# A sparse two-layer graph kernel: value gathers that add into the rows of x while they land

## The chip, the cores and the metric

The kernel runs on one core of a Trainium2 chip. The metric is the device time of one launch in microseconds (us); lower is better. Three runs of the kernel before gave 1190.85, 1191.04 and 1189.97 us, a median of 1190.85 us.

## The reference

Two graph layers over 4096 nodes with 512 features and a random sparse adjacency (some ten neighbours a node). What matters, cut short:

```python
h = jnp.maximum(_layernorm(x), 0.0)
Q, K, V = (h @ W.T for W in (WQ, WK, WV))           # 8 heads of 64
attn = softmax(Q @ K^T * SCALING + energy, masked by adj)
hard = (attn == attn.max(-1, keepdims=True)) / 8      # the best neighbour of each head
x = x + einsum('hqk,hkd->hqd', hard, V)               # layer 0
h = jnp.maximum(_layernorm(x), 0.0)
agg = (adj > 0) @ h / degree
x = x + relu(concat(h @ W_self + b_self, agg @ W_nb + b_nb) @ W_comb + b_comb)   # layer 1
```

Layer 0 gives each node, for each of eight heads, the value row of its single best neighbour, divided by eight. So layer 0 is a search for the best neighbour and a sum of x with eight slices of 64 values. That sum is what the change is about.

## The kernel before

It has three stages.

1. **Lists (0 to about 305 us).** The adjacency is packed into words and decoded to lists of neighbours. Keys, values, x and some per-row numbers (the list, its length, the layernorm's scale and shift) go to one wide table in DRAM, `K_d`: a row holds value, key, numbers, x. The nodes are sorted by degree, so that the 32 tiles of 128 nodes have capacities from 24 neighbours down to 5 (`CAPS`, L512).
2. **Layer 0 and the products of layer 1 (about 305 to 905 us).** A loop over `i` from -5 to 31 (L1652) takes the tiles in the order `turns`: 0, 1, 24, 2, 25, 3, 26, 14, 4, 27, 5, 15, 6, 16, 7, and so on, the last four being 28 to 31. In step `i` it scores the tile `turns[i]` and does earlier or later work of other tiles.
3. **Aggregation (about 905 us to the end).** Rows of `G_d` (layer 1's neighbour product, written in stage 2) are gathered and summed on VectorE for 24 tiles, eight tiles are summed by TensorE through 0/1 masks, and the output is written.

In stage 2 the tiles are of two kinds. The 14 tiles of large capacity (0 to 13) are **apart**: only keys are gathered for their neighbours, and the values are fetched after the winners are known, with eight indirect gathers of 128 rows by 64 floats, one for each head (`value_gathers`, L1221). The other 18 are **fused**: key and value come in one gather of 1025 floats, and the winners are picked by predicated copies on VectorE (L1290).

The names and lines that the steps below touch:

- `rows(r)`, L1162: gathers the tile's own rows, called in step `i` for `turns[i + 5]`. For 25 of the tiles they land in `km`, a tile of 1088 floats a row out of a ring of **eight** (`bufs=8`, L1171). It holds the key, the numbers and, in its last 512 columns, x itself; these columns are called `xg`. The other seven (`wide`) tiles use a part of `room`.
- `query_norm`, L1175: ScalarE reads the list, the numbers and `xg`.
- `scores`, L1238, `winners`, L1266: VectorE multiplies and reduces, group by group of up to four neighbours, then finds the best. For an apart tile the result is `vi`, the row numbers for the value gathers (L1312).
- `value_gathers`, L1221: eight gathers into columns of `o`, a ring of three. They are queued on POOL alternately with the key gathers of a later step (L1671 to L1676).
- `layer1_xo`, L1315: VectorE adds `xg` and `o` into `xo` (L1318, 128 by 512), and SyncE stores `xo` to `X1_d` (L1319). Called by `layer1_stats`.
- `layer1_stats`, L1321: ScalarE sums `xo` (L1332), its squares (L1333) and takes the square root (L1334).
- `layer1_inverse`, L1346: one reciprocal on VectorE (L1348). It is recorded inside `scores` of the same step, behind the first group of neighbours.
- `layer1_norm`, L1350: five ScalarE instructions, L1355 to L1359; the last one reads `xo` and writes the normalised row. It is the last reader of `xo`.
- `layer1_turn`, `layer1_copy`, `layer1`: transposes and products of layer 1.

Every engine works its instructions in the order recorded here (`manual_schedule`), and semaphores keep the order between engines. A tile taken from a ring waits until all readers of an earlier holder of its place are done, also where these are recorded later in the same step. POOL issues the indirect gathers one after another from one queue; a waiting gather holds up all behind it. On that queue each gather also waits for the one eight places before it to have landed, because there are eight semaphores for it.

The order of a step, shortened:

```python
a, b = on(key_gathers, i), late(value_gathers, "value", i)   # POOL
on(rows, i + 5)                                              # POOL: a km from the ring
...
if i >= 0 and turns[i] in fused:
    own_values(turns[i])                                     # POOL
...
late(layer1_stats, "stats", i)                               # VectorE sum, ScalarE sums
...
scores(turns[i], within)                                     # VectorE; the reciprocal inside
on(winners, i)
late(layer1_norm, "stats", i)                                # ScalarE
```

The `plan` (L1591) says in which step a tile has its stats: tiles 0, 24, 1, 25, 2, 26, 3 in steps 3 to 9, and so on, one in a step.

Of the kernel before, what the change touches and what calls it, by code (L numbers as in the profile page):

```python
# [9 lines left out]
F32 = mybir.dt.float32  # L10
# [3 lines left out]
ALU = mybir.AluOpType  # L14
# [4 lines left out]
P = 128  # L19
D = 512  # L20
NC = D // P
H = 8
HD = D // H
# [502 lines left out]
def stats_of(nc, pool, x, mv):  # L526

    st = pool.tile([P, 6], F32, tag="st_s", name="st_s")
    nc.vector.bn_stats(st, x)
    nc.vector.bn_aggr(mv, st)  # L530
# [14 lines left out]
def sparse_path(  # L545
# [4 lines left out]
    nc = tc.nc  # L550
# [560 lines left out]
    with ExitStack() as pb:  # L1111
        bp = pb.enter_context(tc.tile_pool(name="sb", bufs=2))
        xp = pb.enter_context(tc.tile_pool(name="sbx", bufs=8))
# [6 lines left out]
        def gather(dst, src, idx, at=0):  # L1120
            last[0] = nc.gpsimd.indirect_dma_start(  # L1121
                out=dst, out_offset=None, in_=src,
                in_offset=bass.IndirectOffsetOnAxis(ap=idx, axis=0), element_offset=at,
            )
            if at:

                beyond.append(last[0])
                for w in written:
                    tc.declare_no_dep(last[0].ins, w.ins, reason="other columns")
# [32 lines left out]
        def rows(r):  # L1162

            if r in wide:
                k = (wide.index(r) - len(wide)) % OWNS
                own = big[:, OWN0 + k * VKX : OWN0 + (k + 1) * VKX]
                gather(own, K_d[:, :], perm[:, r : r + 1])
                km = own[:, D:VKX]
                st[r]["own"] = own
            else:  # L1170
                km = xp.tile([P, ROWX], F32, tag="km", name="km", bufs=8)  # L1171
                gather(km, K_d[:, :], perm[:, r : r + 1], D)
            st[r].update(km=km, xg=km[:, M_X:ROWX])
# [46 lines left out]

        def value_gathers(r):  # L1221
            s = st[r]
            s["o"] = xp.tile([P, D], F32, tag="o", name="o", bufs=3)
            return [(s["o"][:, ts(h, HD)], V_h, s["vi"][:, h : h + 1]) for h in range(H)]


        V_h = K_d.rearrange("n (a d) -> (n a) d", d=HD)

        def own_values(r):

            s = st[r]
            if r in wide:
                s["o"] = s["own"][:, 0:D]
            else:
                s["o"] = xp.tile([P, D], F32, tag="o", name="o", bufs=3)
                gather(s["o"], K_d[:, :], perm[:, r : r + 1])
# [77 lines left out]

        def layer1_xo(r):  # L1315
            s = st[r]
            s["xo"] = xp.tile([P, D], F32, tag="xo", name="xo", bufs=2)
            nc.vector.tensor_tensor(s["xo"], s["xg"], s["o"], ALU.add)  # L1318
            nc.sync.dma_start(X1_d[ts(r, P), 0, :], s["xo"])  # L1319

        def layer1_stats(r, by_vector=False):  # L1321

            s = st[r]
            if "xo" not in s:
                layer1_xo(r)
            xo = s["xo"]
            if not by_vector:

                q = bp.tile([P, 8], F32, tag="q1", name="q1", bufs=3)

                junk = bp.tile([P, D], F32, tag="hn1", name="hn1", bufs=3)
                nc.scalar.activation(junk, xo, AF.Copy, scale=-1.0 / D, accum_out=q[:, 0:1])  # L1332
                nc.scalar.activation(junk, xo, AF.Square, bias=q[:, 0:1], accum_out=q[:, 1:2])  # L1333
                nc.scalar.activation(q[:, 2:3], q[:, 1:2], AF.Sqrt, bias=epsb, scale=1.0 / D)  # L1334
                nc.scalar.activation(q[:, 3:4], q[:, 1:2], AF.Identity, bias=epsh, scale=-0.5 / D)
                s.update(xo=xo, sq=q, hn=junk)
                return
            mv = bp.tile([P, 2], F32, tag="mv1", name="mv1")
            stats_of(nc, bp, xo, mv)
            v = bp.tile([P, 1], F32, tag="v1", name="v1")  # L1340
            nc.vector.tensor_scalar(v, mv[:, 1:2], EPS, None, ALU.add)
            rs = bp.tile([P, 1], F32, tag="rs1", name="rs1")
            nc.scalar.activation(rs, v, AF.Sqrt)
            s.update(xo=xo, mv=mv, v=v, rs=rs)
# [307 lines left out]
        for i in range(-5, KT):  # L1652
# [16 lines left out]
            if i == 1:  # L1669
                wN = bp.tile([P, NC, D], F32, tag="swN", name="swN", bufs=1)  # L1670
            a, b = on(key_gathers, i), late(value_gathers, "value", i)  # L1671
            while a or b:
                for q, n in ((a, max(1, round(len(a) / max(1, len(b))))), (b, 1)):
# [26 lines left out]
            words_turn()  # L1700
            hot_some(i)
            late(layer1_stats, "stats", i)
            on(query_norm, i + 4)
            late(layer1_out, "move", i)
# [31 lines left out]
        for r in before:  # L1736
            layer1_turn(r)
            tail_turn(r)
        late(layer1_xo, "stats", KT)
        late(layer1_stats, "stats", KT, True)  # L1740
        late(layer1_norm, "stats", KT)
        for r in early[-1:]:
# [40 lines left out]
    with ExitStack() as pd:  # L1783
# [71 lines left out]
        s = ahead  # L1855
# [39 lines left out]
def kernel(tc, *args):  # L1895
    left = sparse_path(tc, *args)
    with tc.If(left > 0):
        general_path(tc, *args)
# [40 lines left out]
```

## Time and profile before

One execution was profiled. Its own time was 1188.29 us and its span 1186.5 us; the median of the three runs without a profile is 1190.85 us.

| What | us |
|---|---|
| Profiled execution, time | 1188.29 |
| Profiled execution, span | 1186.5 |
| TensorE busy over the span | 1023.9 (86%) |
| VectorE busy | 982.7 (83%) |
| POOL busy | 715.1 (60%) |
| ScalarE busy | 550.1 (46%) |
| 112 value gathers `o<-K_d,vi`, POOL busy | 108.1 |
| 32 sums `xo`, VectorE busy (25 from `km`, 7 from `room`) | 17.2 and 4.8 |

How to read the lines: engines are PE (TensorE), DVE (VectorE), ACT (ScalarE), POOL (GpSimd) and SP (SyncE). A line of the timeline has its start and length in us, the engine, the source line, the operation, and output<-inputs; in brackets stands the idle time of the engine just before, and what ended it. "issue" there means that the engine waited for nothing that the profile shows. Line numbers are those of the kernel before.

### The profile page before, as it was taken

The numbers are of one execution on the slowest core, as the hardware profiler recorded it, in microseconds if no ns is written. First come the engines' busy times: TensorE is split into PE (matmuls) and PEld (weight loads), VectorE is DVE, ScalarE is ACT, GpSimd is POOL, SyncE is SP. The second block draws the span as 40 slices with busy tenths as digits, with TensorE's granted clock in tenths as the row PEclk, the third lists the DMA queues.
The fourth block names the chain that finished last, engine by engine and source line by source line (L and its number), as shares of the span: only waits on it lengthen the run. The fifth ranks groups of instructions, "written<-read, shape, count | busy, mean of one in ns | idle before, by whom it ended". The sixth has DMA issues, their size and how long they took to land. (4 is left out here: it accounts for less than half of the span.)

```text
span 1186.5 us, 11454 instructions
## 1 busy us (share of the span) xinstructions
PE 1023.9 (86%) x3079; PEld 501.6 (42%) x3079; DVE 982.7 (83%) x1548; ACT 550.1 (46%) x1222; POOL 715.1 (60%) x939
## 2 busy tenths in 40 slices
PE   3999999979599668688879989888989999999792
PEld 1555555644244224344334434444434444444340
DVE  4358789889289798798989999999983699998894
ACT  3777777932222377486567678754462100000000
POOL 3332323312677757757777777777713777777774
PEclk9999999989799878889889889888999999999996
DMA  9999999979797678889898889988865888888973
GB/s 353 418 420 418 413 418 375 396 226 293 229 269 251 180 233 261 255 278 292 281 289 281 284 280 298 291 279 280 284 256 171 306 310 275 321 288 276 369 242 108
DMA packets 115594, 348.44 MB, mean 294 GB/s; under 512 B 21472, under 2 KB 23552, under 8 KB 107328
## 3 DMA queue, kind: packets, MB, share of 16 engines
q0 software_dynamic: 60560, 201.01, 53.0%
q1 hardware_dynamic: 50560, 146.56, 32.5%
q10 hardware_dynamic: 4400, 0.05, 0.3%
q8 instruction: 26, 0.43, 0.1%
q14 instruction: 48, 0.39, 0.1%
HBM read 287.75 MB, written 64.00 MB: 296 GB/s over the span
## 5 line engine op out<-in xcount | busy, mean ns | idle before, releaser
L1805 PE MATMUL da<-gk,mk 128*128 128x512 f32 x512 | 223.2, 599 | 6.9 <-DVE mk L1556 6.2
L1121 POOL DMA_INDIRECT room<-G_d,sidx x174 | 168.5, 969 | 84.6 <-issue 80.7
L636 PE MATMUL q<-wq,hqT 128*128 128x512 f32 x256 | 151.0, 745 | 51.3 <-DVE pr L1244 51.3
L1250 DVE TENSOR_REDUCE sc<-pr 128x32 f32<-128x2048 f32 (+3 forms) x114 | 183.3, 1608 | 3.8
L1121 POOL DMA_INDIRECT kg<-K_d,sidx x161 | 153.4, 953 | 49.0 <-issue 40.2
L1830 DVE TENSOR_REDUCE acc<-room 128x512 f32<-128x4096 f32 (+5 forms) x23 | 153.0, 6651 | 32.5 <-DMA room<-G_d,sidx 30.6
L1805 PEld LDWEIGHTS da<-gk,mk 128*128 128x128 f32 x512 | 98.2, 192 | 131.9 <-issue 123.1
L1121 POOL DMA_INDIRECT room<-K_d,sidx x118 | 111.6, 945 | 42.9 <-issue 25.6
L1121 POOL DMA_INDIRECT o<-K_d,vi x112 | 108.1, 965 | 34.2 <-issue 32.0
L636 PE MATMUL pk<-wk,room 128*128 128x512 f32 x256 | 118.5, 606 | 2.6 <-ACT room L821 2.6
L636 PE MATMUL pv<-wv,room 128*128 128x512 f32 x256 | 112.6, 592 | 0.0
L636 PEld LDWEIGHTS q<-wq,hqT 128*128 128x128 f32 x256 | 59.2, 243 | 123.0 <-issue 77.7
L1244 DVE TENSOR_TENSOR pr<-q,kg 128x2048 f32<-128x2048 f32 (+3 forms) x47 | 93.3, 1985 | 11.2 <-DMA kg<-K_d,sidx 10.1
L1393 PE MATMUL pr<-swS,hT 128*128 128x512 f32 x216 | 97.1, 592 | 0.0
L636 PE MATMUL pg<-swN,hT 128*128 128x512 f32 x216 | 97.1, 593 | 0.0
L760 ACT ACTIVATE mkt<-adjt,sgb 128x2048 bf16<-128x2048 int32 x44 | 88.0, 1999 | 2.1 <-POOL adjt L678 2.1
L1244 DVE TENSOR_TENSOR pr<-q,room 128x2048 f32<-128x2048 f32 (+3 forms) x42 | 73.2, 1744 | 18.1 <-DMA room<-K_d,sidx 16.0
L636 PEld LDWEIGHTS pv<-wv,room 128*128 128x128 f32 x256 | 48.3, 190 | 59.3 <-issue 59.1
L636 PEld LDWEIGHTS pk<-wk,room 128*128 128x128 f32 x256 | 47.5, 196 | 51.5 <-issue 47.8
L830 DVE SCALAR_TENSOR_TENSOR ks<-pk,swe 128x512 f32<-128x512 f32 x32 | 21.9, 686 | 52.5 <-PE pk L636 46.8
L1517 ACT ACTIVATE hot<-ramp,code 128x256 bf16<-128x256 bf16 x105 | 52.5, 500 | 22.5 <-DVE code L1498 22.5
L779 PE MATMUL pw<-mkt,planes 128*128 128x256 bf16 x512 | 62.8, 277 | 0.0
(254 smaller groups left out, 1619.5 us busy)
## 6 DMA issues: line engine op xcount, KB each, us to landing
adjt<-adj_dram SPq DMA_DIRECT2D x44, 1024.0 KB, 10.4
room<-adj_dram SPq DMA_DIRECT2D x20, 1024.0 KB, 11.0
x<-X_d SPq DMA_DIRECT2D x25, 512.0 KB, 7.8
xt<-x_dram SPq DMA_DIRECT2D x32, 256.0 KB, 8.1
K_d<-ks POOLq DMA_DIRECT2D x32, 256.0 KB, 6.5
X_d<-xo SPq DMA_DIRECT2D x32, 256.0 KB, 4.5
G_d<-gs SPq DMA_DIRECT2D x32, 256.0 KB, 3.9
gk<-G_d SPq DMA_DIRECT2D x16, 512.0 KB, 4.8
```

What stands on the lines that cost most here:

```text
L636: nc.tensor.matmul(dst, h[:, c, :], w[:, c, :], start=(c == 0), stop=(c == NC - 1))
L760: nc.scalar.activation(mk, st[t]["adj"][j], AF.Sigmoid, bias=sgb, scale=400.0, accum_out=degs[:, t, j : j + 1],)
L779: nc.tensor.matmul(pw, planes[:, s, :], st[t]["mk"][j][:, ts(i, SEG)], start=False, stop=(s == NPL - 1),)
L830: nc.vector.scalar_tensor_tensor(ks.rearrange("p (h d) -> p h d", h=H), st[t]["pk"].rearrange("p (h d) -> p h d", h=H), HD**-0.5, web.unsq ...
L1121: last[0] = nc.gpsimd.indirect_dma_start(out=dst, out_offset=None, in_=src, in_offset=bass.IndirectOffsetOnAxis(ap=idx, axis=0), element_o ...
L1244: nc.vector.tensor_tensor(pr[:, :g, :], s["q"].unsqueeze(1).to_broadcast([P, g, D]), kk[:, :, 0:D], ALU.mult)
L1250: nc.vector.tensor_reduce(sc[:, g0 : g0 + g, :], pr[:, :g, :].rearrange("p g (h d) -> p g h d", h=H), AX.X, ALU.add,)
L1393: nc.tensor.matmul(pr, s["hT1"][:, c, :], wS[:, c, :], start=False, stop=(c == NC - 1 and mine is None and not open_))
L1517: nc.scalar.activation(one, ramp, AF.Square, bias=code[:, 0, k : k + 1])
L1805: nc.tensor.matmul(dacc[r], masks[s][:, r, h, :], keys[s][:, h, :], start=(s == 0 and h == 0), stop=(s == NPL - 1 and h == 1),)
L1830: nc.vector.tensor_reduce(acc, g[:, 0:n, :].rearrange("p n f -> p f n"), AX.X, ALU.add)
```

## The change

The eight value gathers of an apart tile no longer write to a tile `o`. They are issued with an add as compute operation and land on the tile's own x, the columns `xg` inside its `km`. After the eight have landed, `xg` is the sum. The VectorE sum of these 14 tiles is left out, and so are their tiles `o` and `xo`. The store to `X1_d`, the three ScalarE readers of stats and norm now read `km`. The 18 fused tiles keep their sum. The store, up to now marked done by the presence of `xo`, is marked by `put`.

```diff
         def gather(dst, src, idx, at=0):
             last[0] = nc.gpsimd.indirect_dma_start(
                 out=dst, out_offset=None, in_=src,
+                **({"compute_op": ALU.add} if src is V_h else {}),
                 in_offset=bass.IndirectOffsetOnAxis(ap=idx, axis=0), element_offset=at,
             )
...
         def value_gathers(r):
             s = st[r]
-            s["o"] = xp.tile([P, D], F32, tag="o", name="o", bufs=3)
-            return [(s["o"][:, ts(h, HD)], V_h, s["vi"][:, h : h + 1]) for h in range(H)]
+            s["xo"] = s["xg"]
+            return [(s["xg"][:, ts(h, HD)], V_h, s["vi"][:, h : h + 1]) for h in range(H)]
...
         def layer1_xo(r):
             s = st[r]
-            s["xo"] = xp.tile([P, D], F32, tag="xo", name="xo", bufs=2)
-            nc.vector.tensor_tensor(s["xo"], s["xg"], s["o"], ALU.add)
+            if "xo" not in s:
+                s["xo"] = xp.tile([P, D], F32, tag="xo", name="xo", bufs=2)
+                nc.vector.tensor_tensor(s["xo"], s["xg"], s["o"], ALU.add)
             nc.sync.dma_start(X1_d[ts(r, P), 0, :], s["xo"])
+            s["put"] = True
 
         def layer1_stats(r, by_vector=False):
 
             s = st[r]
-            if "xo" not in s:
+            if "put" not in s:
                 layer1_xo(r)
```

## The prediction, made before the changed kernel ran

> **What bounds the kernel now.** I began with stage 2, where the change lies, and asked of each engine whether it waits. First the windows view (length, then busy time and count of PE, PEld, DVE, ACT, POOL, then clock, DMA share, GB/s).
>
> ```profile
> core 0: us, PE busy (x) PEld busy (x) DVE busy (x) ACT busy (x) POOL busy (x), PEclk, DMA share, GB/s
> ...
> 516.00:690.00 174.00, 146.38 (x413) 70.49 (x412) 160.82 (x194) 118.15 (x314) 131.91 (x139) 0.89 0.89 284
> 690.00:830.00 140.00, 124.62 (x342) 59.58 (x341) 134.25 (x174) 93.48 (x256) 106.17 (x112) 0.90 0.90 284
> ```
>
> POOL looks three quarters busy, but a gather of 0.945 us is always followed by 0.30 us of issue, and 139 x 1.25 = 174 us and 112 x 1.25 = 140 us: the queue has no gap between 516 and 830 us. VectorE is 92% and 96% busy in them. Two full engines, so the question is which one waits for the other. The timeline of POOL shows the gathers of own rows (`km`):
>
> ```profile
> 423.32 0.94 POOL L1121 DMA_INDIRECT km<-K_d,perm  x1 [6.80 <-DVE xo L1318]
> 441.18 0.94 POOL L1121 DMA_INDIRECT km<-K_d,perm  x1 [0.30 <-issue]
> ...
> 483.23 0.94 POOL L1121 DMA_INDIRECT km<-K_d,perm  x1 [0.30 <-issue]
> ...
> 516.02 0.94 POOL L1121 DMA_INDIRECT km<-K_d,perm  x1 [8.14 <-DVE xo L1318]
> ```
>
> The only two long holes of the queue between 342 and 859 us stand here: a row gather waits until the sum at L1318 has freed a place in the ring of `km`. And the timeline of VectorE shows its waits for gathers:
>
> ```profile
> 485.82 2.29 DVE L1244 TENSOR_TENSOR pr<-q,room 128x2048 f32<-128x2048 f32 x1 [5.09 <-DMA room<-K_d,sidx]
> ...
> 829.69 1.76 DVE L1244 TENSOR_TENSOR pr<-q,room 128x1536 f32<-128x1536 f32 x1 [1.06 <-DMA room<-K_d,sidx]
> ...
> 855.59 2.29 DVE L1244 TENSOR_TENSOR pr<-q,room 128x2048 f32<-128x2048 f32 x1 [0.35 <-DMA room<-K_d,sidx]
> ```
>
> At 855.59 VectorE still waits for a gather issued by a queue that has run without a gap since 516.02. So POOL sets the time up to there; then VectorE's last three and a half tiles end at 893, the last products follow, and the gathers of stage 3 start at 905.44. What moves POOL's start at 516 moves all of that, and stage 3 with it.
>
> **The change, part by part.**
>
> *Removed: 14 sums.* Each is 0.69 us by its row, 0.60 from its start to the next one's (436.88 to 437.48): 8.4 us of VectorE. Of these, 12 lie before 829.69, where VectorE then waits for a gather, so they lengthen a wait and give nothing. Two lie behind it (839.38 and one at 852.64), and the wait at 855.59 takes up those 1.2 us. I count 0; if POOL did not bind, it would be 8.4.
>
> *Removed: tiles `o` and `xo` of 14 tiles.* Gathers into `o` wait in the profile for nothing but issue (116 times 0.30 us), so their places are not short: 0.
>
> *Moved: the release of `km`.* Until now an apart tile's `km` is free after L1318. Now its last reader is the norm on ScalarE (L1359), and the store to `X1_d` reads it too. In the changed program as built, the row gathers of steps 3, 5, 7 and 9 wait for exactly this: the norm and the store of tiles 0, 1, 2 and 3, where they waited for the sum. (Step 4, the hole at 423.32, follows tile 24, which is fused: unchanged. Later apart holders have their stats steps ahead, and only their stores are waited for: 0.) The norm comes late because its reciprocal (L1348) stands on VectorE behind the first group of the step's scores:
>
> ```profile
> 443.44 0.15 DVE L1348 RECIPROCAL q<-q 128x1 f32<-128x1 f32 x1
> ...
> 515.07 0.68 DVE L1318 TENSOR_TENSOR xo<-km,o 128x512 f32<-128x512 f32 x1
> ...
> 521.64 0.15 DVE L1348 RECIPROCAL q<-q 128x1 f32<-128x1 f32 x1
> ```
>
> ```profile
> 444.94 0.81 ACT L1359 ACTIVATE hn<-xo,q 128x512 f32<-128x512 f32 x1
> ...
> 522.38 0.18 ACT L1355 ACTIVATE q<-q 128x1 f32<-128x1 f32 x1
> ...
> 523.67 0.81 ACT L1359 ACTIVATE hn<-xo,q 128x512 f32<-128x512 f32 x1
> ```
>
> - Step 3: tile 0's norm ends at 398.55, the gather is at 408.06. No wait.
> - Step 5: tile 1's norm ends at 445.75. Without the sum the reciprocal is 0.60 earlier: 445.15. From release to the gather's start POOL takes 0.27 (515.75 to 516.02). So 445.42 in place of 441.18: **+4.24 us**. The store, issued by 437.6 with 4.5 us to landing, is done before. Behind the gather wait the fused rows of step 6; VectorE waits for these by 466.98 (2.16 us, `o`), 476.06 (2.60) and 485.82 (5.09), so it slips by the same 4.24.
> - Step 7: POOL arrives at 487.47; tile 2's norm ended at 482.89, and 4.24 - 0.60 + 0.27 later is 486.8. No wait.
> - Step 9: the reciprocal at 521.64 becomes 521.64 + 4.24 - 0.60 = 525.28, ending 525.43. ScalarE waited 1.47 us for the sum in this step and no longer does, so its chain starts at once, 0.04 later; from L1355 to the norm's end it takes 524.48 - 522.38 = 2.10: 527.57, and POOL at 527.84 in place of 516.02. The stall has grown from 8.14 to 15.7, and the shift in all is **+11.8 us**, the 4.24 among it.
>
> Behind that gather wait the key gathers of tile 5 and then everything. VectorE has 9.3 us of waits between 529 and 830 and eight sums (4.8 us) less to do there, none of which helps a queue that is full.
>
> *Changed: 112 gathers add.* No row of this trace adds while landing. POOL's time for a gather doesn't follow the width (0.94 to 0.95 us for 64, 513 and 1088 floats), so an extra price would be one for each row's descriptors. From below: 0. From above, the nearest rows are two plain writes of 128 and of mostly 640 to 1024 rows:
>
> ```profile
> L729 POOL DMA_DIRECT2D K_d<-s x4: 548/554/582, 30.9 to 32.6; - x4
> ...
> L933 POOL DMA_DIRECT2D K_d<-meta x5: 929/944/997, 140.0 to 297.7; - x5
> ```
>
> (944 - 554) ns for 512 further rows is 0.76 ns a row, 0.10 us for 128. A farther bound is all that an indirect gather costs above a direct write, 0.945 - 0.554 = 0.39 us. I take the middle of 0 and 0.10, 0.05 us. On the path are 80 gathers behind 516, some 15 between 441 and 485, some 14 before 407: 109 x 0.05 = **+5.4 us** (0 to 10.9; by the far bound 42.5). The Trainium skill ("Collectives: The Full Stack", section "The bandwidth ceiling: the fold count and why AG ≠ RS ≠ AR") says that an add in the DMA needs two source reads and so two read descriptors for each chunk; it speaks against the change. Taken as an estimate with the row above, three descriptors in place of two are half a row's price, 64 x 0.76 = 0.05 us and 5.3 us in all; no run here shows it.
>
> Landing: value gathers land after 2.4 to 7.4 us (median 4.4), and the queue looks back eight gathers, 10.0 us. Their readers stand a step behind: tile 13's last gather lands near 847.5, its ScalarE sum was at 853.35. I count 0 up to a landing of 10 us.
>
> *Sum:* 11.8 + 5.4 = 17.2. On the profiled execution 1188.29 + 17.2 = 1205.5; on the median, 2.56 us above it, 1190.85 + 17.2 = **1208 us**. Its own range, from the two ends of the add's price: 1203 to 1214.
>
> **The rivals.**
>
> *The adds cost POOL far more, or land late.* For it: nothing in the trace shows an add, and the queue has no slack. Against it: width costs nothing now. At 0.39 us each, 11.8 + 42.5 gives 1245. If a landing took 12 us, the look back of eight would set a pace of 12/8 = 1.5 us for 160 gathers, the 80 value gathers behind 516 and as many between them: 0.25 x 160 = 40, and 1243.
>
> *VectorE takes up part of the stall.* For it: from 667.4 to 829.7 it never waits, so it might be the late one, and 8.4 us of its work goes. Then the end moves by 11.8 - 8.4 = 3.4: 1194. Against it: at 829.69 and 855.59 it waits for gathers, so its lead is nil there.
>
> *Faster: VectorE is the bound and the removed sums count in full.* One mechanism, at 516 to 830 us: 14 x 0.60 = 8.4, 1182. It decides if the row gathers don't wait longer, that is if the norms end before POOL reaches them (440.88) or where it already waits (515.75). They end at 445 and 524.
>
> **How the numbers follow.** Forecast 0.67; costlier or late adds 0.20, spread from 1214 up; VectorE takes up a part 0.08; faster 0.05. The range goes from 1197, which leaves out the faster case and half of the partial one, to 1236, which leaves out the upper half of the costly case: about 0.19 outside. A measurement of this kernel can tell 0.2%, some 2.4 us, from no change. Faster 0.05; within 0.2%: 0.03, from the partial case; slower 0.92.
>
> **What would show it.** Right: the row gather of step 5 begins behind ACT's norm with some 5 us idle, that of step 9 with 15 to 16; POOL without gaps after that; VectorE waits for `room` and `kg` more than 9 us longer in all; stage 3 starts some 17 us later and is as long as before; the value gathers at about 1.0 us. Wrong: row gathers without new waits, or a start of stage 3 that moves by less than 8 us. A value gather at 0.945 takes 5.4 us off the sum; one at 1.3 makes the second case.

## The result, and the profile after

The changed kernel took 1266.38 us (median of four runs, 1264.42 to 1267.2) beside 1190.41 us of the kernel before (1188.65 to 1191.04): 1.0638 times as long, 95% interval 1.062 to 1.0657, or 76 us more. The prediction was 1208, its range ended at 1236. The profiled execution took 1267.2 us with a span of 1265.5, so 78.9 and 79.0 us more than the one of before. Line numbers behind L1123 are now one to three higher: the sum is L1320, the reciprocal L1351, the norm L1362.

One more fact is needed to read some of the experiments: on two other chips the kernel before takes 1460 to 1469 us, and on one of these, where the change ran as it is, it is a gain. They have a section of their own.

The row of the value gathers, of the group view (busy us in all, mean ns of one, idle time before):

```profile
L1121 POOL DMA_INDIRECT km<-K_d,vi x112 | 174.4, 1557 | 34.1 <-issue 32.0 <-DMA room<-K_d,sidx 0.9 <-DMA km<-K_d,vi 0.9
```

Before, the same 112 gathers took 108.1 us, 965 ns each. An add while landing costs POOL 0.592 us, 66.3 us over all. Their median landing is 4.3 us after, 4.4 before (the longest 6.3 after, 7.4 before): nothing lands late.

POOL's timeline, which before had its two long holes at 423.32 and 516.02:

```profile
432.23 0.94 POOL L1121 DMA_INDIRECT km<-K_d,perm  x1 [5.46 <-DVE xo L1320]
...
454.35 0.94 POOL L1121 DMA_INDIRECT km<-K_d,perm  x1 [4.89 <-ACT hn L1362]
455.59 0.94 POOL L1121 DMA_INDIRECT room<-K_d,sidx  x1 [0.30 <-issue]
456.84 1.56 POOL L1121 DMA_INDIRECT km<-K_d,vi  x1 [0.30 <-issue]
458.71 0.96 POOL L1121 DMA_INDIRECT room<-K_d,sidx  x1 [0.30 <-issue]
459.98 1.54 POOL L1121 DMA_INDIRECT km<-K_d,vi  x1 [0.30 <-issue]
...
545.30 0.94 POOL L1121 DMA_INDIRECT km<-K_d,perm  x1 [15.05 <-ACT sidx L1265]
```

Two things are to be seen. From the start of an adding gather to the next start it is 1.87 and 1.84 us, where it was 1.25. And there are three holes now: step 4's (5.46), a new one in step 5 (4.89, until the norm), and step 9's (15.05, was 8.14). The releaser named at 545.30 is ScalarE's next instruction; the norm itself ends at the same moment, as ScalarE's timeline shows:

```profile
453.27 0.81 ACT L1362 ACTIVATE hn<-km,q 128x512 f32<-128x512 f32 x1
...
544.22 0.81 ACT L1362 ACTIVATE hn<-km,q 128x512 f32<-128x512 f32 x1
544.94 0.27 ACT L1265 CAST sidx<-room 128x4 int32<-128x4 f32 x2
```

454.08 and 545.03 are the ends of these norms (start plus length); the row gathers follow 0.27 us later, the latency that the prediction used. Before, step 9's norm ended at 524.48.

The windows of the same stretches of stage 2 as before:

```profile
516.00:690.00 174.00, 131.36 (x355) 62.72 (x353) 139.47 (x172) 102.84 (x272) 124.33 (x115) 0.86 0.83 248
690.00:830.00 140.00, 112.02 (x313) 55.26 (x313) 114.58 (x145) 97.51 (x260) 110.61 (x97) 0.87 0.87 249
```

From 690 to 830 POOL issues 97 instructions where it issued 112, in a queue as full as before; VectorE, which was busy for 134.25 us of these 140, now is for 114.58. The share of the DMA engines falls too, from 0.89 and 0.90 to 0.83 and 0.87, so they are no busier than before. What VectorE does with the rest stands in its waits, from 340 us to the end of stage 2 (total us, times, longest), first before, then after:

```profile
DVE pr L1244 <- DMA room<-K_d,sidx: 16.0, 7, 5.1
DVE pr L1244 <- DMA kg<-K_d,sidx: 9.2, 4, 3.3
...
DVE o L1290 <- DMA o<-K_d,perm: 2.2, 1, 2.2
```

```profile
DVE pr L1245 <- DMA room<-K_d,sidx: 86.0, 23, 8.5
DVE o L1291 <- DMA o<-K_d,perm: 20.9, 4, 6.6
DVE pr L1245 <- DMA kg<-K_d,sidx: 12.9, 4, 4.6
```

The key gathers, which queue between the adding gathers, arrive late. Stage 3 starts at 983.73 in place of 905.44, 78.3 us later, and is as long as it was, 281.77 us beside 281.06:

```profile
983.73:1265.50 281.77, 249.66 (x580) 109.73 (x578) 229.16 (x117) 7.82 (x13) 204.12 (x216) 0.96 0.80 275
```

So the trace gives a first division of these 78.3 us: 66.3 us of dearer gathers, and 25.4 us of holes (5.46, 4.89, 15.05) in place of 15.2 (6.80, 0.30, 8.14), 10.2 more: 76.5 together. Over the whole of stage 2, from 305 us on, POOL is busy 68.6 us longer (414.53 before, 483.10 after) and idle 9.7 us longer, and that is the 78.3; most of what the first division lacks are the plain gathers into `room`, 958 ns each for 945. The experiments were to tell whether this holds when one of the two is alone.

### The profile page after: what moved, and what is told of

It reads as the page before. It is cut to its first block, busy times and chain, and to the rows that moved or that the text cites. A ratio compares the mean times of both kernels' runs of the same rounds, so it can differ in the third digit from the quotient of the medians.

```text
span 1265.5 us, 11466 instructions
## 1 busy us (share of the span) xinstructions
PE 1036.0 (82%) x3079; PEld 506.6 (40%) x3079; DVE 972.9 (77%) x1534; ACT 550.0 (43%) x1222; POOL 786.2 (62%) x939
## 2 busy tenths in 40 slices
DMA packets 128140, 348.45 MB, mean 275 GB/s; under 512 B 35808, under 2 KB 37888, under 8 KB 119872
## 3 DMA queue, kind: packets, MB, share of 16 engines
q0 software_dynamic: 73104, 201.01, 52.6%
## 4 chain that ended last, share of the span: by engine, by line
PE 25%; DVE 23%; DMA 19%; POOL 19%; issue 11%; ACT 3%; POOLq 0%; DVEq 0%; ACTq 0%
POOL km L1121 7%; POOL room L1121 7%; PE pk L636 7%; PE da L1808 7%; DVE pr L1245 6%; DMA kg<-K_d,sidx 5%; DMA room<-K_d,sidx 4%; DVE sc L1251 4%; PE pw L779 3%; PE pv L636 3%; POOL kg L1121 3%; DMA room<-G_d,sidx 3%; PE pr L1396 2%; DVE room L1291 2%; DVE o L1291 2%
## 5 line engine op out<-in xcount | busy, mean ns | idle before, releaser
L636 PE MATMUL q<-wq,hqT 128*128 128x512 f32 x256 | 162.9, 795 | 111.4 <-DVE pr L1245 111.4
L1121 POOL DMA_INDIRECT km<-K_d,vi x112 | 174.4, 1557 | 34.1 <-issue 32.0
L636 PEld LDWEIGHTS q<-wq,hqT 128*128 128x128 f32 x256 | 63.6, 261 | 192.9 <-DVE pr L1245 98.1
L1291 DVE COPY_PREDICATED o<-best,room 128x512 f32<-128x512 int32 x67 | 49.3, 735 | 23.1 <-DMA o<-K_d,perm 20.9
```

What stands on the lines that cost most here:

```text
L636: nc.tensor.matmul(dst, h[:, c, :], w[:, c, :], start=(c == 0), stop=(c == NC - 1))
L1121: last[0] = nc.gpsimd.indirect_dma_start(out=dst, out_offset=None, in_=src, **({"compute_op": ALU.add} if src is V_h else {}), in_offset=b ...
L1291: nc.vector.copy_predicated(s["o"].rearrange("p (h d) -> p h d", h=H), best[:, k, :].bitcast(I32).unsqueeze(2).to_broadcast([P, H, HD]), b ...
```

## The experiments

Theory A: the added 76 us are some 65 us of POOL's time for the adds and some 12 us of later release of `km`. Its rivals: the waits make most of it, since a held row gather holds the whole queue (R); the add burdens the DMA engines or lands late (D); VectorE takes a part up (V).

### The later release alone

```diff
-            s["xo"] = xp.tile([P, D], F32, tag="xo", name="xo", bufs=2)
+            s["xo"] = s["xg"] if r not in fused else xp.tile([P, D], F32, tag="xo", name="xo", bufs=2)
             nc.vector.tensor_tensor(s["xo"], s["xg"], s["o"], ALU.add)
```

> The kernel before with the apart tiles' sum in place in km, so that norm and store free it, and no add. Theory A: the row gathers of steps 5 and 9 begin at 446.0 and 529.6 in place of 441.18 and 516.02, 13.6 us more: 1202 to 1204 us. Rival R: 1240 or more. Rival V (VectorE takes the stall up): 1195 or less.

Measured: 1200.18 us beside 1187.19 of the kernel before on that chip, 13.0 us more (ratio 1.0104, interval 1.0085 to 1.0123). POOL's timeline:

```profile
444.92 0.94 POOL L1121 DMA_INDIRECT km<-K_d,perm  x1 [5.14 <-DVE pr L1244]
...
527.55 0.94 POOL L1121 DMA_INDIRECT km<-K_d,perm  x1 [16.01 <-DVE sc L1273]
```

The profile names VectorE instructions as releasers, but ScalarE's timeline has the ends of the two norms 0.27 us ahead of these gathers, at 444.65 and 527.28:

```profile
443.84 0.81 ACT L1359 ACTIVATE hn<-km,q 128x512 f32<-128x512 f32 x1
...
526.47 0.81 ACT L1359 ACTIVATE hn<-km,q 128x512 f32<-128x512 f32 x1
```

Both row gathers stand within 2.1 us of where the norm was expected to let them (446.0 and 529.6). Stage 3 starts 15.2 us later than in the profile of the kernel before. The time is 2 us below the 1202 to 1204 that were named, which had counted from a slower kernel before; the difference, 13.0, is what tests the working. Rivals R and V are out for the release: it costs what its two waits cost, and it is a sixth of the loss. That leaves 76.0 - 13.0 = 63.0 us for the adds, where theory A has some 65.

### Release and adds apart, on a slower queue

These four carry two small memsets on POOL behind every gather, which makes stage 2 longer for all of them alike. The memsets were meant to make POOL's queue the bound on the other kind of chip too; the four ran on one chip of the first kind, where the kernel before takes 1188.43 us. "Nine" means nine places for `km` in place of eight, so that no row gather waits for a norm; the room for it comes from other tiles, in lines not shown here.

```diff
+            for _ in range(2):
+                nc.gpsimd.memset(gap, 0.0)
             if at:
...
-                km = xp.tile([P, ROWX], F32, tag="km", name="km", bufs=8)
+                km = xp.tile([P, ROWX], F32, tag="km", name="km", bufs=9)
```

> pad_all with nine places for km, as in before_nine: the base for the adds alone. The holes of 3.0 and 2.4 us at 441 and 544 us go: Theory A 1315 to 1319 us.

> The changed kernel with the memsets of pad_all and nine places for km: against padall_nine it holds the adds alone. Theory A: 64 us above padall_nine, some 1381. Rival R: within 20 us of padall_nine. Rival S: not above padall_nine.

> pad_all with the sum of the apart tiles in place in km, as in release_alone: the later release alone, with no add. Theory A: step 5's row gather 1.9 us later, step 9's 10.4 later in all: 1331 us. Rival R: 1360 or more. Rival V (VectorE takes it up): 1324 or less.

> The changed kernel with the two memsets of pad_all behind every gather; it is compared with pad_all (1320.9 us). Theory A: 109 x 0.59 = 64 us for the adds and some 9 us for the release (step 5's row gather would wait until 463.8 in place of 462.24, step 9's until 553.5 in place of 544.36): 1394 us. Rival S (a slower queue is still a gain on these chips): 1321 or less. Rival R (the release makes most of it): the same 1394, but then padall_release is near it.

| Kernel | median us | ratio to before, interval |
|---|---|---|
| padall_nine | 1322.40 | 1.1125 (1.1102 to 1.1148) |
| padall_after_nine | 1390.56 | 1.1705 (1.1681 to 1.1729) |
| padall_release | 1330.99 | 1.1197 (1.1173 to 1.1221) |
| padall_after | 1395.67 | 1.1742 (1.1719 to 1.1765) |

The adds alone: 1390.56 - 1322.40 = 68.2 us (expected 64). In these two the only hole of POOL's queue above 2 us behind 305 us is the one ahead of stage 3, so no wait of a row gather is in that number. The release alone against pad_all (the kernel before with the two memsets, 1320.92 on a chip of the other kind): 10.1 us (expected 10). Both: 74.8 (expected 73). That pad_all ran elsewhere weakens the last two. Against padall_nine, on the one chip, the release is 8.6 us, and both are 73.3: with the adds in it the release costs only 5.1 us (padall_after less padall_after_nine), so the two parts do not quite add up. In padall_after, POOL comes later to its row gathers, and one hole is left (11.57 us) where padall_release has three (4.16, 2.46, 12.04). The expectation for padall_nine, 1315 to 1319, was missed: the holes of 3.0 and 2.4 us that pad_all has are closed, and the time is not lower; as pad_all did not run on this chip, what they were worth stays open.

### POOL's time without an add

```diff
+            if src is V_h:
+                for _ in range(5):
+                    nc.gpsimd.memset(gap, 0.0)
             if at:
```

> The kernel before with five memsets on POOL behind each of the 112 value gathers (0.57 us of POOL's time in place of the 0.59 of an add), no add and the release as before. Theory A: 1188 to 1190 and 109 x 0.57 = 62 us, 1251 us. Rival D (an add costs by its second read in the DMA engines, not by POOL's time): within 20 us of the kernel before. Rival R (waits for the norm make most of the 76 us): the same as rival D.

Measured: 1281.79 us beside 1187.19, 94.6 more (ratio 1.0799, interval 1.0776 to 1.0823), well above the 62 expected. POOL's timeline shows why:

```profile
700.45 0.94 POOL L1121 DMA_INDIRECT o<-K_d,vi  x1 [0.30 <-issue]
701.40 0.74 POOL L1127 MEMSET gap<- 128x1 f32 x5
702.76 0.94 POOL L1121 DMA_INDIRECT room<-K_d,sidx  x1 [0.63 <-issue]
704.01 0.95 POOL L1121 DMA_INDIRECT o<-K_d,vi  x1 [0.30 <-issue]
```

Five memsets take 0.74 us and not 0.57, and the gather behind them waits 0.63 and not 0.30. Over the 112 value gathers the mean from start to next start is 2.13 us, before 1.27: 0.86 x 112 = 96 us. So the price of the dummy work was misjudged, but POOL's time without any add gives the loss that this time amounts to. Rival D is not needed, and R, which expected at most 20 us here, is out here too.

### A ruler for the price of an add

```diff
+            n = P // 2 if r < 7 else P
-            return [(s["xg"][:, ts(h, HD)], V_h, s["vi"][:, h : h + 1]) for h in range(H)]
+            return [(s["xg"][:n, ts(h, HD)], V_h, s["vi"][:n, h : h + 1]) for h in range(H)]
...
-                gather(s["o"], K_d[:, :], perm[:, r : r + 1])
+                nc.scalar.mul(s["o"], s["xg"], 0.0)
+                n = P // 2 if 24 <= r < 28 else P
+                gather(s["o"][:n], K_d[:, :], perm[:n, r : r + 1], 0, n == P)
```

> The changed kernel as a ruler for single gathers; rows 64 to 127 of tiles 0 to 6 get no values and rows 64 to 127 of tiles 24 to 27 no own value. Read is POOL's time for one gather: an add of 64 rows by 64 floats (tiles 0 to 6), an add of 128 rows by 64 floats (tiles 7 to 13), an add of 128 rows by 512 floats onto zeros (own values of the non-wide fused tiles but 24 to 27), a plain gather of 64 rows by 512 floats (tiles 24 to 27). Theory A, the price is one further descriptor for a row, whatever its width: 1.54 us for 128 by 64 and for 128 by 512 alike, and 1.54 less 64 x 4.6 ns = 1.25 us or less for 64 rows. Rival W, the price goes by bytes: 0.95 + 8 x 0.59 = 5.7 us at 512 floats. Rival F, the price is fixed for an instruction that adds: 64 rows cost 0.59 us more than a plain gather of 64 rows. The time of the whole kernel says nothing here.

The last argument of `gather` says here whether it adds. The run met the other kind of chip; the adds of 128 rows by 64 floats take 1.53 to 1.56 us there, as in the changed kernel. POOL's timeline (a plain gather of 64 rows by 512 floats, an add of 64 rows by 64, an add of 128 rows by 512, an add of 128 rows by 64):

```profile
555.17 0.91 POOL L1121 DMA_INDIRECT o<-K_d,perm  x1 [0.30 <-issue]
...
593.79 1.41 POOL L1121 DMA_INDIRECT km<-K_d,vi  x1 [0.30 <-issue]
...
596.78 1.54 POOL L1121 DMA_INDIRECT o<-K_d,perm  x1 [0.30 <-issue]
...
945.61 1.54 POOL L1121 DMA_INDIRECT km<-K_d,vi  x1 [0.30 <-issue]
```

Eight times the bytes cost nothing: 1.54 at 64 and at 512 floats, so rival W (5.7 us) is out. Half the rows save 0.13 us of an add and 0.04 of a plain gather (0.95 to 0.91). The surcharge is therefore 0.50 us at 64 rows and 0.59 at 128. A straight line through these two points, an estimate, has some 1.4 ns a row on some 0.41 us that do not depend on the rows. That is nearer to rival F (fixed for an instruction) than to my own theory of one price a row, which wanted 1.25 or less for 64 rows. What POOL does in this time the profile does not show.

### Half of the heads

```diff
+            s["o"] = xp.tile([P, D], F32, tag="o", name="o", bufs=3)
+            return [
+                ((s["o"], s["xg"])[h % 2][:, ts(h, HD)], V_h, s["vi"][:, h : h + 1], 0, h % 2 == 1)
+                for h in range(H)
+            ]
```

> The changed kernel, but only the four odd heads add while landing; the four even heads land in a tile o as before and VectorE adds these 256 columns into x inside km. Same release as in the change. Theory A: half of the price of the adds, 54.5 x 0.59 = 32 us, plus the release, 12 to 13 us: 1190.4 + 45 = 1235 us; the gathers to o take 0.95 us and those to km 1.54. Rival Q (an add slows its neighbours on the queue or lands late, so that the price is not by the gather): near 1266, or gathers to o above 1.0 us. Rival R (waits): above 1255.

This met the other kind of chip, so its time (1402.93 us) tests nothing of the sum. The group view does what was asked of it for rival Q:

```profile
L1121 POOL DMA_INDIRECT km<-K_d,vi x56 | 87.0, 1554 | 17.1 <-issue 16.5 <-DMA room<-K_d,sidx 0.6
L1121 POOL DMA_INDIRECT o<-K_d,vi x56 | 53.9, 963 | 17.1 <-issue 16.2 <-DMA room<-K_d,sidx 0.6 <-DVE pr L1249 0.3
```

Adding and plain gathers stand side by side in one queue, 1554 and 963 ns, where they took 1557 and 965 when all eight added or none did: the price goes by the gather, and the plain ones between them pay nothing.

### The other chips

release_alone, before_nine, after_nine and half_heads were to divide the loss directly.

> The kernel before with nine places for km instead of eight. The room comes from one place less for hn1 and for xo; the sums of tiles 12, 13 and 28 to 31, whose km is never used again, go into x inside km. A row gather then takes a place that was freed a step earlier, so the holes of 6.8 us and 8.1 us in POOL's queue at 423 and 516 us should close. Theory A (POOL's queue sets the time of stage 2): 1190.4 less 10 to 15 us, 1175 to 1180. Rival V (VectorE takes it up): 1187 to 1190. It may be a version that beats both.

> The changed kernel with the same nine places for km and the same ways to make room, so no row gather waits for a norm. Against the run with nine places of the kernel before it holds the adds alone. Theory A: 109 x 0.59 = 64 us above that run, 1239 to 1244 us, some 23 to 27 us below the changed kernel. Rival R (waits make most of the loss): within 30 us of that run. In both the value gathers take 1.54 us.

They met a chip on which the kernel before takes 1466 us, and none of these expectations applied: release_alone (the kernel of "The later release alone") 1465.82 (twice more, one of them on a second such chip, 1468.9 and 1468.38), before_nine 1470.16, half_heads 1402.93, after_nine 1355.91. The later release costs nothing there, nine places bring nothing, and the more gathers add, the faster it is. The profile of release_alone on such a chip, windows (columns as before):

```profile
570.00:600.00 30.00, 20.63 (x65) 10.84 (x63) 19.97 (x22) 17.47 (x48) 17.93 (x19) 0.84 0.66 209
614.00:634.00 20.00, 0.00 (x0) 0.00 (x0) 0.00 (x0) 0.00 (x0) 13.28 (x14) 0.59 0.76 236
640.00:660.00 20.00, 17.90 (x56) 9.58 (x56) 19.45 (x22) 18.38 (x48) 10.49 (x11) 0.79 0.58 177
```

For 20 us TensorE, VectorE and ScalarE do nothing at all, while POOL goes on issuing gathers, up to 631.4 us. In stage 2 of this profile the three stand still together 14 times for over 3 us (3.5 to 20), 135 us in all; in that of the kernel before at the head of this document they do so once, for 3.3 us, though POOL's queue runs there without a gap for over 300 us. In stage 3 TensorE's timeline, in which the matmuls depend on no gather, shows how it begins and ends:

```profile
1161.36 38.46 PE L1805 MATMUL da<-gk,mk 128*128 128x512 f32 x89 [0.68 <-ACT gs L1429]
1201.50 0.59 PE L1805 MATMUL da<-gk,mk 128*128 128x512 f32 x1 [1.67 <-issue]
...
1210.60 1.01 PE L1805 MATMUL da<-gk,mk 128*128 128x512 f32 x1 [1.79 <-issue]
1214.10 1.01 PE L1805 MATMUL da<-gk,mk 128*128 128x512 f32 x1 [2.49 <-issue]
1216.20 1.01 PE L1805 MATMUL da<-gk,mk 128*128 128x512 f32 x1 [1.09 <-issue]
```

POOL issues without a pause from 1166 to 1216 us. TensorE works 89 matmuls at 0.43 us each until 1200, then one in 1.4 to 3.5 us, waiting for nothing that the profile shows; POOL pauses at 1215.7, and from 1220.4 TensorE works 145 matmuls at 0.45 us each again. Theory S: a queue of gathers without a pause holds the other engines after some 30 us, so what slows the queue is a gain there. The change itself, and the memsets alone:

> The changed kernel as it is, beside the kernel before on the same chip, because on the two chips of the last runs the kernel before takes 1466 us and not 1190. There ScalarE stood still some 10 to 35 us at a time with all it waited for done, and went on 2 to 5 us after POOL's queue had paused. Theory S (on these chips ScalarE is held while POOL issues without a pause, so a slower queue holds it less): the changed kernel is not slower there but faster, 1350 to 1380 us. Theory A alone (POOL's queue is the bound on every chip): 1466 + 76 = 1542 us. On a chip where the kernel before takes 1190 us both expect 1266.

> The kernel before, with five small memsets on POOL (0.11 us each by their row) behind each of the 112 value gathers: 0.57 us of POOL's time in place of the 0.59 that an add costs, and no add, no other release, no other packet. Theory A (what the adds cost is POOL's time and nothing else): where the kernel before takes 1190 us, 109 x 0.57 = 62 us more, 1252. Rival D (the add's second read burdens the DMA engines or its landing): within 20 us of the kernel before. Where the kernel before takes 1466 us, theory S expects 1360 to 1420 from the slower queue alone, and rival D no gain.

after_again: 1356.17 us beside 1468.72, ratio 0.9253 (0.9205 to 0.9301). pad (the kernel of pad_b): 1367.72, ratio 0.9331 (0.9286 to 0.9376). Dummy work on POOL brings nearly all that the adds bring. Next, bytes or issue, and how the pauses should lie:

```diff
-                gather(gg[:, i, :], G_d[:, :], sidx[:, ds(sat[r] + i + 1, 1)])
+                gather(gg[:, i, 0:HD], G_d[:, :], sidx[:, ds(sat[r] + i + 1, 1)])
```

> The kernel before, but the 174 gathers of stage 3 fetch 64 floats of each row of G_d in place of 512, so the neighbours' sums lack the other columns. POOL's issue stays as it is, an eighth of the gathered bytes moves. Read is the pace of the matmuls of stage 3 while POOL issues without a pause, on a chip where the kernel before takes 1466 us. Theory I (issue by POOL holds the engines): TensorE still falls to one matmul in 1.4 to 3.5 us after some 30 us of unbroken issue. Rival B (the bytes in the DMA queues hold them): TensorE runs at 0.43 us a matmul through stage 3, which is 60 us shorter or more. Where the kernel before takes 1190 us stage 3 stays as long as it is or is up to 30 us shorter.

Measured: 1473.43 us in its one execution, beside 1460.23. TensorE's timeline in stage 3 has the same pattern as above: 91 matmuls at 0.43 us, then, 34 us after POOL's issue began at 1169.3, one in 1.4 to 3.5 us, and from 1223.3, behind POOL's pause at 1218.4, 127 matmuls at 0.45 us. An eighth of the bytes in stage 3 shortens nothing, so there it is not the bytes (rival B is out). The number of gathers and of rows stayed, so issue by POOL (theory I) fits, but nothing tells it from the number of rows.

```diff
+            rest[1] += 1
+            if rest[1] % 20 == 0:
+                for _ in range(8):
+                    nc.gpsimd.tensor_scalar(rest[0], rest[0], 1.0, None, ALU.mult)
```

> The kernel before, with a rest of some 4 us (eight small tensor_scalar on POOL) behind every 20th gather of stages 2 and 3. On the chips where the kernel before takes 1466 us, TensorE, VectorE and ScalarE stand still together after POOL has issued gathers for some 30 to 40 us without a pause, until it pauses. Theory S2 (the stand-still needs such an unbroken run of issue, and a pause of a few us ends it): 640 gathers give 32 rests, 128 us of POOL's time, but the stand-stills of 10 to 27 us go: 1300 to 1380 us, and no stretch of 10 us without TensorE and VectorE in stage 2. Rival S3 (it goes by POOL's mean pace alone): 128 us over 640 gathers are 0.2 us a gather, a third of what the 112 pads took, twice as many: near the pads' 1368 or above, and stand-stills still there. Where the kernel before takes 1190 us both expect a loss of 60 to 90 us.

> The kernel before, with two memsets of 0.11 us on POOL behind every indirect gather of stages 2 and 3, 0.23 us in each, some 100 us of POOL's time in stage 2 and 40 in stage 3, spread evenly. On the chips where the kernel before takes 1466 us: by S3 (the mean pace decides) as fast as the rests or faster, 1300 to 1370 us; by S2 (only a pause of a few us helps) above 1440. Where the kernel before takes 1190 us: 1280 to 1300.

pause: 1324.84 us, ratio 0.9069 (0.9 to 0.9138); pad_all: 1320.92, ratio 0.9032 (0.8966 to 0.9098). Both beat both kernels there. S2 (only a pause of a few us helps) falls with pad_all, which spreads its rests evenly and is as fast; S3 (the mean pace decides) fits pad_all, but not pause, for which it wanted 1368 or more with the stand-stills left: in its profile the three engines stand still together for at most 5 us. What holds the engines inside the chip stays open: the profile names no releaser, and no run here shows one. On the chips of the prediction such rests are a loss (padall_nine, 1322 beside 1188).

## Why the prediction was wrong

*POOL's queue bounds stage 2.* Right. Behind 545.30 the queue of the changed kernel has one hole of over 2 us up to stage 3's wait (6.6 us at 939, where there were 7.3 before), VectorE waits for gathers 98.9 us (`room` and `kg`) in place of 25.2, and stage 3 moves whole: 78.3 us later, as long as before.

*14 sums removed, counted 0.* Right as far as it can be seen: VectorE has 9.8 us less to do (982.7 to 972.9) and waits 74 us longer for `room` and `kg`.

*The release of `km`.* Right in the steps that it counted: no wait in steps 3 and 7, 4.89 us idle in step 5 (some 5 were predicted), 15.05 in step 9 (15 to 16). It was put at 11.8 us in all; the holes of the trace have grown by 10.2, since the one of step 4, counted as unchanged, shrank from 6.80 to 5.46 as POOL came to it 10 us later, with 16 adds ahead of it. The release alone, with the sums left in, measures 13.0 where its own working gave 13.6.

*112 gathers add.* This step failed, and it alone makes the miss. I took 0.05 us for an add, the middle of 0 and 0.10, by the slope of plain writes over their rows, and named 0.39 as a far bound. It is 0.592: with the prediction's own 109 gathers on the path 64.5 us in place of 5.4. With the 11.8 of the release that is 76.3; 76.0 was measured. That it fits to 0.3 us is in part luck: in the trace the holes grew by 10.2 and all 112 gathers by 66.3. The reasoning behind the 0.05 was that a gather's time doesn't follow the width, so that a surcharge could only be one for each row's descriptors, and those are cheap. The first half is right (1.54 us at 64 and at 512 floats). The second is not: by the estimate from the ruler most of the surcharge, some 0.41 us, comes with the instruction, and this no row of the trace bounded. The far bound, all that an indirect gather costs above a direct write, was no bound either: it compared two other kinds of transfer, and nothing ties the price of an add to their difference.

The rule from the Trainium skill ("Collectives: The Full Stack", section "The bandwidth ceiling: the fold count and why AG ≠ RS ≠ AR") that an add needs two source reads is not shown by the trace: the bytes of POOL's queue are the same (201.01 MB). What the trace shows is another packing. Packets under 512 B went from 21472 to 35808, 14336 more, which is one for each of 112 x 128 rows, while 1792 packets of 2048 B are gone, and 1792 x 8 = 14336: eight rows of a plain gather stand in one packet, each row of an adding gather in its own. Whether that is what costs POOL its time no run shows. The estimate that I made from the rule, 0.05 us an add, did not hold: 0.592 was measured.

*Landing, counted 0.* Right, a median of 4.3 us beside 4.4.

*The rivals.* "The adds cost POOL far more" is what happened; it had a chance of 0.20 and its own price was too low (1245). The late landing in the same case did not. "VectorE takes up a part" and "the removed sums count in full" are out: VectorE waits throughout. The range left out the upper half of the costly case; with an unseen operation on a queue without slack, a price of the order of the instruction itself (0.95 us) would have been a better upper end, 11.8 + 109 x 0.95 = 115 us.

## What to carry to other kernels

Before an operation moves into a DMA that one engine issues, ask what the issue costs on that engine, and whether its queue has slack: here an instruction of 0.69 us on an engine that had to wait anyway was traded for 8 x 0.59 us on the one that set the time. If no row of the profile shows the new form, bound its price by the whole instruction that it is a variant of and not by a slope; a ruler of one gather of each kind would have settled it. And when a buffer's last reader changes, look up who waits for its place: that part could be worked out from the trace to within 2 us.

## What the runs showed of the hardware that was not expected

- An indirect gather that adds takes POOL 1.54 us for 128 rows and 1.41 for 64, a plain one 0.95 and 0.91; 64 or 512 floats a row make no difference. The median landing is 4.3 us, a plain one's 4.4.
- Five memsets of 128 by 1 behind a gather hold the queue for 0.74 us and delay the next gather by 0.33 more, 0.86 us in the mean where their rows alone gave 0.57.
- On two of the chips TensorE, VectorE and ScalarE stand still together for up to 20 us at a time (release_alone) once POOL has issued gathers for 25 to 39 us without a pause, and mostly resume 1 to 5 us after it pauses. The kernel before takes some 275 us more there; 135 us of such stand-stills were counted in stage 2, and how the rest comes about was not worked out. In stage 3 it does not depend on the bytes (narrow3). On the one of the two where it ran, the change is a gain: 0.9253 there, 1.0638 here. A time from one chip is not the time on every chip.
